# Fusing a distance-biased attention and an int4 map into one software-pipelined loop in written order

## The chip, the cores and the metric

The kernel runs on one core of a Trainium2 chip. A core has a tensor engine (PE, with its weight loads shown apart as PEld), a vector engine (DVE), a scalar engine (ACT), GpSimd (POOL) and a queue engine (SP) that issues most of the DMA transfers. The metric is device time in microseconds of a whole execution: median of three runs 1596.04 us, from 1595.28 to 1596.16.

## What is computed

The reference is a two-layer decoder with a layer norm after every residual, on 16 batches of 128 tokens of 256 numbers. Six parts follow each other, and the kernel has a stage for each:

```python
x = layernorm(x + moe(x))                    # stage 0: 8 experts, top 2, quantised weights
x = layernorm(x + attention(x, ctx, dist))   # stage 1: 16 heads of 16 numbers
x = layernorm(x + int4_map(x))               # stage 2
x = layernorm(x + state_space(x))            # stage 3
x = layernorm(x + attention(x, ctx, mask))   # stage 4
x = layernorm(x + expert_choice(x))          # stage 5
```

The parts that matter here, cut to their core:

```python
# stage 1
q = (query @ Wq.T + bq) * d ** -0.5;  k = ctx @ Wk.T + bk;  v = ctx @ Wv.T + bv
scores = einsum('bhqd,bhkd->bhqk', q, k) - log(distances + 1e-9) * abs(distance_scaling)
out = softmax(scores) @ v
return out @ Wo.T + bo
# stage 2
w = clip(round(kernel / scale), -8, 7) * scale       # scale = max(abs(kernel)) / 7
return x @ w + bias + (x @ a) @ b
```

## The kernel before

Everything is float32 in the stages concerned. A batch is one tile `x[b]` of 128 tokens (partitions) by 256. The instructions are traced in Python order, and a scheduler then chooses the order of each engine's instructions by its own costs and priorities, unless a block asks for the written order. An engine executes its list in order, each instruction waiting for the semaphores of what it needs.

**End of stage 0.** The experts' outputs are rows in a DRAM tensor `y_dram`. For each batch two indirect DMAs on POOL (L503) gather the two rows of every token into a tile of the tag `y`; DVE adds them with their weights (L507) and takes statistics (L508, L509); after four batches POOL computes the scales (L82, L83: power −0.5), and DVE normalises (L514). With `issue_after`, later gathers are held behind the scales of the group before.

**Stage 1** runs over 16 batches, in groups of four. `keys(g, c)` projects the context of four batches to keys; each key row is written twice (`mine`), once for the even and once for the odd head of a pair, the other head's rows zeroed, so that 32-row matmuls serve two heads (L623, L627). `values(b)` does the same for values (L634, L636), into one of three rotating tiles that hold zeros in the other head's columns. `turn(g)` transposes `x` (L101, L106), `queries(g)` projects it (L614, L615). `weights(b)` computes the scores (L649: four row groups of the array in turn), adds the bias `-log(dist)` (L655), takes the row maximum (L660) and exponentiates head by head (L662). `turn_weights(b)` transposes the 16 blocks of weights (L669) and copies them back in four pieces, two on DVE (L671) and two on ACT (L673). `attend1(b)` multiplies by the values (L680) and, with the constant matrix `sums`, adds up the weights (L688); DVE takes the reciprocal of 128x256 sums (L693) and multiplies (L695). `finish(b)` projects (L700), adds the residual (L702 on POOL, L703) and normalises (L88 to L93). The loop works on batch `b`, `b-1` and `b-2` in a turn, so three batches are in flight.

**Stage 2** comes after it: the int4 weights from the largest magnitude (L756 to L775), then for each batch a transposition, a product (L781), the residual (L783 on POOL, L784) and the normalisation.

[...]stage 1 has two tiles of two banks for the scores (`ps_s`), two banks `ps_m`, one `ps_t`, one `ps_o`. The weights of stages 3 and 4 (`load3`, `load4`) are loaded when the memory of stage 0 comes free; SP issues them from 271.28 us on.

Of the kernel before, what the change touches and what calls it, by code (L numbers as in the profile page):

```python
# [19 lines left out]
P = 128  # L20
# [98 lines left out]
def stage0(K, ahead):  # L119
# [3 lines left out]
    with ExitStack() as ctx:  # L123
# [152 lines left out]
        y_dram = K.new(dram, [NE * CAP, D], F32, "y_dram")  # L276
# [16 lines left out]
        for k in range(2):  # L293
# [4 lines left out]
            i = K.new(keep, [P, NB], U32, f"idx{k}")  # L298
# [3 lines left out]
            w = K.new(keep, [P, NB], F32, f"wt{k}")  # L302
# [189 lines left out]
        after = None  # L492
        for b0 in range(0, NB, 4):
            st = K.new(small, [P, 4, 6], F32, "ln_st4")
            mv = K.new(small, [P, 4, 2], F32, "ln_mv4")
            for i in range(4):
                b = b0 + i
                if i % 2 == 0:
                    g = K.new(work, [P, 5, D], F32, "y", bufs=2)
                for k in range(2):  # L500
                    gk = g[:, 2 * (i % 2) + k, :]
                    with tc.issue_after(after.ins) if after is not None and i >= 2 else ExitStack():
                        nc.gpsimd.indirect_dma_start(  # L503
                            out=gk, out_offset=None, in_=y_dram[:],
                            in_offset=bass.IndirectOffsetOnAxis(ap=idx[k][:, b:b + 1], axis=0),
                        )
                    nc.vector.scalar_tensor_tensor(x[b], gk, wt[k][:, b:b + 1], x[b], ALU.mult, ALU.add)  # L507
                nc.vector.bn_stats(st[:, i, :], x[b])  # L508
                nc.vector.bn_aggr(mv[:, i, :], st[:, i, :])  # L509
            rs = K.new(small, [P, 4], F32, "ln_rs4")  # L510
            after = K.rsqrt(small, rs, mv[:, :, 1:2].rearrange("p b c -> p (b c)"), 1.0, 1e-5, "ln_t4")
            for i in range(4):
                b = b0 + i
                nc.vector.tensor_scalar(x[b], x[b], mv[:, i, 0:1], rs[:, i:i + 1], ALU.subtract, ALU.mult)  # L514
# [36 lines left out]
def stage1(K, w, ctxT):  # L551
    tc, nc = K.tc, K.nc
    x = K.x
    with ExitStack() as ctx:
# [4 lines left out]
        ps = ctx.enter_context(tc.tile_pool(name="s1_ps", bufs=2, space=PSUM))  # L559
# [4 lines left out]
        nc.vector.memset(tiny, 1e-9)  # L564
        nds = K.new(keep, [P, 1], F32, "nds")
        nc.vector.tensor_scalar(nds, w.scale, -1.0, None, ALU.mult)
        nc.vector.tensor_tensor(nds, nds, w.scale, ALU.min)
        for g in range(4):
            bg = bias[:, 4 * g:4 * g + 4, :]
            nc.scalar.activation(bg, bg, AF.Ln, bias=tiny)  # L570
            nc.vector.tensor_scalar(bg, bg, nds, None, ALU.mult)


        pi = K.new(keep, [P, 1], I32, "pi")
        nc.gpsimd.iota(pi, pattern=[[0, 1]], base=0, channel_multiplier=1)
        nc.vector.tensor_scalar(pi, pi, 4, 1, ALU.logical_shift_right, ALU.bitwise_and)
        mine = K.new(keep, [P, 2], F32, "mine")
        nc.vector.tensor_copy(mine[:, 1:2], pi)
        nc.vector.tensor_scalar(mine[:, 0:1], mine[:, 1:2], -1.0, 1.0, ALU.mult, ALU.add)
        bq = K.new(keep, [P, KD], F32, "bq")  # L580
        nc.vector.tensor_scalar(bq, w.bq, HD ** -0.5, None, ALU.mult)
        bk = K.new(keep, [P, KD, 2], F32, "bk")
        for c in range(KD):
            nc.vector.tensor_scalar(bk[:, c, :], mine, w.bk[:, c:c + 1], None, ALU.mult)

        sums = K.new(keep, [P, 2, 2, HD], F32, "sums")
        nc.vector.memset(sums, 0.0)
        for j in range(2):
            nc.vector.memset(sums[:, j, j, :], 1.0)

        vals = [K.new(keep, [P, NH, 2, HD], F32, f"vals{i}") for i in range(3)]
        for t in vals:
            nc.vector.memset(t, 0.0)

        bo = K.new(keep, [P, D], F32, "bo_all")
        pb = K.new(ps, [P, D], F32, "ps_m")
        for k in range(KD):
            nc.tensor.matmul(
                pb, w.bv[:, k:k + 1].to_broadcast([P, P]), w.o[:, k, :], start=(k == 0), stop=(k == KD - 1),
            )  # L600
        nc.vector.tensor_tensor(bo, w.bo, pb, ALU.add)

        xT, qT, kT, s, oT = {}, {}, {}, {}, {}

        def turn(g):
            xT[g] = K.new(grp, [P, KD, 512], F32, "xT")
            K.transposed(ps, xT[g], x[4 * g:4 * g + 4], "ps_m")

        def queries(g):
            qT[g] = K.new(grp, [P, KD, 512], F32, "qT")  # L610
            for c in range(KD):
                pq = K.new(ps, [P, 512], F32, "ps_m")
                for k in range(KD):
                    nc.tensor.matmul(pq, w.q[:, k, c * P:(c + 1) * P], xT[g][:, k, :], start=(k == 0), stop=(k == 1))  # L614
                nc.scalar.activation(qT[g][:, c, :], pq, AF.Identity, scale=HD ** -0.5, bias=bq[:, c:c + 1])  # L615


        def keys(g, c):
            if c == 0:
                kT[g] = K.new(grp, [P, KD, 2, 512], F32, "kT")  # L620
# [90 lines left out]
        for b in range(NB + 2):  # L711
            g, i = divmod(b, 4)
            if b < NB:
                weights(b)
# [977 lines left out]
```

## Time and profile before

The profiled execution lasted 1598.8 us, at a mean granted PE clock of 0.922. The edges of the stages, from the timeline of the trace:

| stretch | us | PE busy | DVE busy | ACT busy | POOL busy |
|---|---|---|---|---|---|
| int4 map with the first squares of stage 3 | 480 to 521 | 27.84 | 21.02 | 13.06 | 23.87 |
| start of stage 3 | 521 to 560 | 24.35 | 29.96 | 12.11 | 5.27 |
| state space and memory | 560 to 780 | 203.71 | 148.39 | 88.75 | 99.38 |
| mostly attention with mask | 780 to 1179 | 375.80 | 193.05 | 186.01 | 95.78 |
| expert choice | 1179 to 1598 | 391.49 | 84.83 | 69.27 | 20.07 |

How to read the views that follow: the page gives, for 40 slices of some 40 us, the busy share of each engine in tenths, and the granted PE clock in tenths of full speed. An answer by stretches gives busy time and, in brackets, the number of instructions of each engine. A line of the timeline has start, duration, engine, source line, operation, output and inputs by the program's names, and in square brackets how long the engine was idle before and what released it. Matmuls are pipelined and their ends are modelled: a busy PE is not a PE at its peak. The start of one piece to the start of the next is the better measure, and the weight loads (PEld) show it.

### The profile page before, as it was taken

Reading aid. Unit: us, or ns where it says so; the run is one execution under the profiler, and the core shown is the slowest. Engines: PE = TensorE matmul, PEld = TensorE weight load, DVE = VectorE, ACT = ScalarE, POOL = GpSimd, SP = SyncE. Lnnn points to the kernel's source line nnn. Section 1 sums busy time; section 2 is a strip of 40 time slices with the busy share of each in tenths; the row PEclk is TensorE's granted clock in tenths of the full one; section 3 lists DMA queues with packets and bytes.
Section 4 is the critical chain, followed back from the end, with each engine's and each line's share of the span. In section 5 each row is a group of like instructions: output and inputs, shape, how many; then the busy total and the mean of one; then the engine's idle time right before and its main releaser. Section 6 shows DMA issues by size and latency. Waiting matters only on the chain. (4 is left out here: it accounts for less than half of the span.)

```text
span 1598.8 us, 18940 instructions
## 1 busy us (share of the span) xinstructions
PE 1355.1 (85%) x6925; PEld 887.7 (56%) x6925; DVE 823.8 (52%) x1692; ACT 630.3 (39%) x1642; POOL 349.7 (22%) x427
## 2 busy tenths in 40 slices
PE   3466645998987599989999999999887999999996
PEld 3243332555544266656655777777675555555554
DVE  4987756776875766774844444444713111131114
ACT  4577742565533344443222655545633111111110
POOL 2113145011115165533023221122311000000003
PEclk9778786999997799999899999999977999999998
DMA  7532125200000000000102100000000222222102
GB/s 240 170 127 96 42 79 97 85 1 1 2 1 1 0 1 1 0 1 1 53 0 107 52 1 1 1 1 1 1 1 0 69 86 92 91 72 79 66 14 66
DMA packets 49357, 71.99 MB, mean 45 GB/s; under 512 B 9552, under 2 KB 39216, under 8 KB 49008
## 3 DMA queue, kind: packets, MB, share of 16 engines
q1 hardware_dynamic: 47088, 65.24, 12.3%
q0 software_dynamic: 2176, 5.55, 1.7%
q8 instruction: 54, 0.88, 0.2%
q14 instruction: 39, 0.32, 0.1%
HBM read 60.77 MB, written 5.80 MB: 42 GB/s over the span
## 5 line engine op out<-in xcount | busy, mean ns | idle before, releaser
L1561 DVE TENSOR_TENSOR h<-h,ps_m 128x512 f32<-128x512 f32 x64 | 44.0, 687 | 254.2 <-PE ps_m L1558 254.2
L82 POOL TENSOR_SCALAR ln_t<-ln_mv 128x1 f32<-128x1 f32 (+1 forms) x84 | 16.3, 194 | 602.0 <-DVE ln_mv L90 592.5
L1558 PE MATMUL ps_m<-xin,l1f_upT 128*128 128x512 f32 x256 | 120.6, 592 | 0.0
L1555 PE MATMUL ps_g<-xin,l1f_gateT 128*128 128x512 f32 x256 | 120.6, 592 | 0.0
L1392 ACT ACTIVATE s<-s,m 128x128 f32<-128x128 f32 x256 | 99.0, 388 | 46.7 <-DVE m L1389 46.4
L1569 PE MATMUL ps_y<-l1f_downT,h 128*128 128x256 f32 x512 | 111.8, 379 | 0.0
L1560 ACT ACTIVATE h<-ps_g 128x512 f32<-128x512 f32 x64 | 38.2, 597 | 176.0 <-PE ps_g L1555 176.0
L1569 PEld LDWEIGHTS ps_y<-l1f_downT,h 128*128 128x128 f32 x512 | 97.3, 190 | 16.6 <-issue 3.8
L1396 POOL TENSOR_TENSOR s<-s,t 128x1024 f32<-128x1024 f32 x32 | 60.7, 1896 | 181.8 <-DVE t L1395 138.0
L662 ACT ACTIVATE s<-s,m 128x128 f32<-128x128 f32 x256 | 78.1, 389 | 40.6 <-DVE m L660 39.2
L1558 PEld LDWEIGHTS ps_m<-xin,l1f_upT 128*128 128x128 f32 x256 | 48.6, 190 | 59.5 <-issue 59.3
L1555 PEld LDWEIGHTS ps_g<-xin,l1f_gateT 128*128 128x128 f32 x256 | 48.6, 190 | 56.5 <-issue 56.0
L1298 PE MATMUL ps_m<-ctxT,l1x_W_k 128*128 128x256 f32 x256 | 61.1, 393 | 5.2 <-ACT ring L1301 4.7
L1423 PE MATMUL ps_m<-half,oT 128*128 128x256 f32 x256 | 61.0, 381 | 0.0
L1318 PE MATMUL ps_m<-l1x_W_v,ctxT 128*128 128x512 f32 x128 | 60.6, 618 | 0.0
L892 DVE SCALAR_TENSOR_TENSOR acc<-ps_m,l1a_conv_w,acc 128x508 f32<-128x508 f32 (+2 forms) x72 | 52.5, 734 | 11.0 <-ACT acc L888 10.9
L1298 PE MATMUL ps_m<-xT,half 128*128 128x256 f32 x256 | 57.5, 383 | 0.7 <-ACT xT L1364 0.7
L1298 PEld LDWEIGHTS ps_m<-ctxT,l1x_W_k 128*128 128x128 f32 x256 | 49.0, 196 | 13.8 <-ACT ring L1301 5.7
L649 PE MATMUL ps_s<-kT,qT 32*128 32x256 f32 x256 | 42.0, 463 | 16.6 <-DVE s L655 16.4
L93 DVE TENSOR_SCALAR x<-r,ln_mv,ln_rs 128x256 f32<-128x256 f32 x64 | 27.8, 435 | 54.6 <-POOL ln_rs L83 54.5
L1574 ACT COPY y<-ps_y 128x256 f32<-128x256 f32 x32 | 11.9, 372 | 110.8 <-PE ps_y L1569 63.1
L1298 PEld LDWEIGHTS ps_m<-xT,half 128*128 128x128 f32 x256 | 47.7, 190 | 8.5 <-ACT xT L1364 1.0
(426 smaller groups left out, 2982.3 us busy)
## 6 DMA issues: line engine op xcount, KB each, us to landing
w<-in_w_gate_dram SPq DMA_DIRECT2D x9, 1024.0 KB, 5.8
l1f_gateT<-in_l1f_gateT_dram SPq DMA_DIRECT2D x8, 1024.0 KB, 5.3
l1f_upT<-in_l1f_upT_dram SPq DMA_DIRECT2D x8, 1024.0 KB, 6.3
l1f_downT<-in_l1f_downT_dram SPq DMA_DIRECT2D x8, 1024.0 KB, 5.6
w<-in_w_down_dram SPq DMA_DIRECT2D x9, 512.0 KB, 6.6
ring<-y SPq DMA_DIRECT2D x128, 32.0 KB, 1.8
y_dram<-y SPq DMA_DIRECT2D x4, 640.0 KB, 3.3
x<-in_x_dram SPq DMA_DIRECT2D x16, 128.0 KB, 2.9
```

The costliest lines, as they stand in the source:

```text
L649: nc.tensor.matmul(pss[r // 2][:, r % 2, c, :, :], qT[g][rows, c, at], kT[g][rows, c, :, at], start=True, stop=True,)
L662: nc.scalar.activation(half[:, i, :], half[:, i, :], AF.Exp, bias=m[:, i:i + 1])
L892: nc.vector.scalar_tensor_tensor(accv[:, :, j:], pcv[:, :, :P - j], w.conv[:, c, TAPS - 1 - j:TAPS - j], accv[:, :, j:], ALU.mult, ALU.add,)
L1298: nc.tensor.matmul(pq[:, j, :], wt[k][:, at], src[:, k, :], start=(k == 0), stop=(k == KD - 1))
L1318: nc.tensor.matmul(pv, self.ctxT[:, k, b * P:(b + 1) * P], self.w.v[:, k, 512 * j:512 * j + 512], start=(k == 0), stop=(k == KD - 1),)
L1392: nc.scalar.activation(half[:, i, :], half[:, i, :], AF.Exp, bias=m[:, i:i + 1], accum_out=t[:, i:i + 1],)
L1396: nc.gpsimd.tensor_tensor(half, half, t.unsqueeze(2).to_broadcast([P, 8, P]), ALU.mult)
L1423: nc.tensor.matmul(py, oT[b][:, c, :], w.o[c // 4][:, c % 4, :], start=(c == 0), stop=(c == NC - 1))
L1555: nc.tensor.matmul(pg, w.gate[:, k, at], xin[:, k, e, :], start=(k == 0), stop=(k == KD - 1))
L1558: nc.tensor.matmul(pu, w.up[:, k, at], xin[:, k, e, :], start=(k == 0), stop=(k == KD - 1))
L1561: nc.vector.tensor_tensor(h, h, pu, ALU.mult)
L1569: nc.tensor.matmul(pd, hid[c][:, g * P:(g + 1) * P], w.down[:, c, :], start=(c == 0), stop=(c == FI // P - 1),)
```

## The change

The gathers' end of stage 0, stage 1 and stage 2 become one stage in which **all engines run in the written order** (`manual_schedule()` without a list of engines).

- `after_experts` returns four functions, `fetch`, `combine`, `scales` and `scaled`, that the new stage calls where it wants them. The tiles that live on (`idx`, `wt`, `y_dram`) move to pools that last longer. Gathers of six batches are issued first; those of batches 12 to 15 go into the first turns of the loop. The gathered rows have three buffers of their own (`got`).
- Keys of groups 0 to 2 and values 0 to 2 are projected ahead of the loop, the rest in turns 0 to 3. All 16 value tiles and all four key tiles are kept, so no buffer rotates. Their room is that of weights needed later: `load3` and `load4` are called after the stage, and each load waits until the last use of what stood there.
- The sums of the weights are no longer matmuls: POOL folds the 128 columns to 16 in three additions (`added`), DVE reduces the rest and takes the reciprocal of 128x16 numbers (`summed`), PE transposes those (`turn_sums`) and spreads them to 128x256 with a matrix of zeros and ones, `each` (`spread`). ACT copies the result to SBUF.
- Scores and bias are done by halves (`scores(b, h)`, `biased(b, h)`), on one score buffer; all four copies of transposed weights are on ACT, `ps_t` has two banks, `ps_m` four.
- Turn `n` of the loop works on five batches: scores and first exponentials of `n`, second exponentials of `n-1`, attention of `n-2`, residual and normalisation of `n-3`, int4 product of `n-4`. There are 20 turns.

It is meant to let the int4 map and the gathers run beside the attention, and to fix an order in which each engine has work of other batches while it waits.

```diff
-def stage0(K, ahead):
+def stage0(K, ahead, late, late_dram):
...
-                    with tc.issue_after(after.ins) if after is not None and i >= 2 else ExitStack():
-                        nc.gpsimd.indirect_dma_start(
...
+    def after_experts(work, small):
...
+        def fetch(b):
+            if b % 2 == 0:
+                got[b // 2] = K.new(work, [P, 4, D], F32, "got", bufs=3)
+            for k in range(2):
+                nc.gpsimd.indirect_dma_start(
...
-        ps = ctx.enter_context(tc.tile_pool(name="s1_ps", bufs=2, space=PSUM))
+        ps = ctx.enter_context(tc.tile_pool(name="s1_ps", bufs=4, space=PSUM))
+        ctx.enter_context(tc.manual_schedule())
+        fetch, combine, scales, scaled = after_experts(work, small)
...
+        parts = [t.rearrange("p a b -> p (a b)") for t in (room.inp, room.out, room.gate, own)]
+        vals = [t[:, 512 * i:512 * i + 512] for t, n in zip(parts, (5, 2, 2, 7)) for i in range(n)]
...
+        kT += [t.rearrange("p k (j n) -> p k j n", j=2) for t in (room.k, room.v)]
...
+        def scores(b, h):
...
+            pss[h] = K.new(ps, [P, 2, 2, 2, P], F32, "ps_s", bufs=1)
             for c in range(KD):
-                for r in range(4):
-                    rows = slice(32 * r, 32 * r + 32)
+                for i in range(2 * h, 2 * h + 2):
+                    rows = slice(32 * i, 32 * i + 32)
...
+        def added(b):
+            at, n = s[b].rearrange("p r c j k -> p (r c j) k"), P
+            while n > HD:
+                n //= 2
+                to = K.new(work, [P, NH, n], F32, f"sum{n}", bufs=1)
+                nc.gpsimd.tensor_tensor(to, at[:, :, :n], at[:, :, n:], ALU.add)
+                at = to
+                yield
+            ts[b] = at
...
-            pd = K.new(ps, [P, KD, P], F32, "ps_m")
-            for j in range(2):
-                for r in range(4):
-                    nc.tensor.matmul(
-                        pd[32 * r:32 * r + 32, :, :], sums[:, j, :, :].rearrange("p j d -> p (j d)"), s[b][:, r, :, j, :],
-                        start=(j == 0), stop=(j == 1),
-                    )
-            ri = K.new(work, [P, KD, P], F32, "ri")
-            nc.vector.reciprocal(ri, pd)
...
+        for b in range(6):
+            fetch(b)
...
+        for n in range(NB + 4):
...
+            if last:
+                residual("r", n - 3)
+                factor("r", n - 3)
+            if old:
+                summed(n - 2)
+                turn_weights(n - 2, 0)
+                turn_weights(n - 2, 1)
+                rest("r", n - 2, bo)
+            if new:
+                scores(n, 0)
+                biased(n, 0)
+            if prev:
+                exp(n - 1, 1, range(0, 2))
+            if old:
+                turned(n - 2, 0)
+                pn = turn_sums(n - 2)
+                turn_weights(n - 2, 2)
+            if prev:
+                exp(n - 1, 1, range(2, 4))
+            if old:
+                turned(n - 2, 1)
+            if last:
+                normed("r", n - 3)
+                rest("r2", n - 3, w2.bias)
+            if new:
+                largest(n, 0)
+            if end:
+                product("r2", n - 4, yT[n - 4], w2.kernel)
+            if prev:
+                exp(n - 1, 1, range(4, 6))
+            if old:
+                nc.scalar.copy(tT[n - 2], pn)
+                turned(n - 2, 2)
+                turn_weights(n - 2, 3)
+            if prev:
+                exp(n - 1, 1, range(6, 8))
+                sums = added(n - 1)
+                next(sums)
+            if old:
+                spread(n - 2)
+                turned(n - 2, 3)
+                nc.scalar.copy(ri[n - 2], pd[n - 2])
...
+            if n < 4:
+                combine(8 + 2 * n)
+            if new:
+                scores(n, 1)
+            if end:
+                residual("r2", n - 4)
+                factor("r2", n - 4)
+            if prev:
+                next(sums)
+                next(sums)
+                next(sums, None)
+            if last:
+                turn_again(n - 3)
+            if old:
+                attend1(n - 2)
+            if new:
+                biased(n, 1)
+                exp(n, 0, range(8))
+            if old:
+                nc.vector.tensor_tensor(oT[n - 2], po[n - 2], ri[n - 2], ALU.mult)
+            banks = []
+            if g < 3 and i == 1:
+                banks = list(turn(g + 1))
+            elif g < 3 and i > 1:
+                banks = list(queries(g + 1, i - 2))
...
+            if last:
+                nc.scalar.copy(yT[n - 3], pt[n - 3, "x"])
+            out_of(banks)
+            for b in ((3, 4, 5, 6), (7, 8, 9, 10), (11, 12, 13), (14, 15))[n] if n < 4 else ():
+                values(b)
+            if new:
+                largest(n, 1)
+            if old:
+                product("r", n - 2, oT[n - 2], w.o)
...
+            if end:
+                normed("r2", n - 4)
...
-def stage2(K, wts):
...
+                after_experts = stage0(K, ahead, late, late_dram)
...
+                stage1(K, w.one, w.two, w.ctxT, room, after_experts)
                 w.three, w.four = load3(K, p3), load4(K, p4)
-                stage1(K, w.one, w.ctxT)
-                stage2(K, w.two)
```

## The prediction

> **What bounds the kernel now.** I read the page's slices first, to see where the tensor engine is starved, then the busy time by stretches to put numbers on the stage that changes.
>
> ```profile
> PE   3466645998987599989999999999887999999996
> DVE  4987756776875766774844444444713111131114
> ACT  4577742565533344443222655545633111111110
> PEclk9778786999997799999899999999977999999998
> ```
> ```profile
> core 0: us, PE busy (x) PEld busy (x) DVE busy (x) ACT busy (x) POOL busy (x), PEclk, DMA share, GB/s
> 242.00:272.00 30.00, 12.55 (x42) 5.59 (x40) 15.81 (x46) 4.86 (x6) 18.83 (x21) 0.63 0.47 71
> 300.00:340.00 40.00, 39.82 (x279) 22.10 (x277) 27.86 (x43) 20.04 (x55) 5.35 (x11) 1.00 0.00 1
> 490.00:510.00 20.00, 13.43 (x45) 9.17 (x44) 9.66 (x31) 6.70 (x30) 14.66 (x29) 0.73 0.00 1
> ```
>
> A slice is 40 us. Stage 0 ends near 215, the int4 stage near 521. Between them lie three different regimes: the row gathers (215 to 272), in which no engine is full; the attention loop (272 to 473), in which PE is full and DVE, ACT and POOL are not; the int4 map (473 to 521), again with no engine full and the PE clock at 0.73. The timeline gives the edges and the cost of small pieces:
>
> ```profile
> 219.15 1.08 POOL L503 DMA_INDIRECT y<-y_dram,idx  x1 [4.62 <-DVE dist L571]
> 220.54 0.95 POOL L503 DMA_INDIRECT y<-y_dram,idx  x1 [0.30 <-issue]
> 258.18 1.19 DVE L655 TENSOR_TENSOR s<-ps_s,dist 128x1024 f32<-128x1024 f32 x1
> 271.70 1.18 DVE L660 TENSOR_REDUCE m<-s 128x8 f32<-128x1024 f32 x1
> 521.11 1.14 DVE L871 TENSOR_SCALAR xn<-x,rs 128x256 f32<-128x256 f32 x4
> ```
> ```profile
> 363.22 0.79 PEld L680 LDWEIGHTS ps_o<-s,vals 128*32 128x32 f32 x26 [0.33 <-DVE ln_st L88]
> 365.07 0.74 PEld L649 LDWEIGHTS ps_s<-kT,qT 32*128 32x128 f32 x14 [0.41 <-issue]
> 366.14 0.30 PEld L623 LDWEIGHTS ps_m<-ctxT,l0x_WkT 128*128 128x128 f32 x2 [0.33 <-issue]
> ```
> ```profile
> ACT s L662 <- DVE m L660: 32.9, 14, 5.4
> ACT s L673 <- PE ps_t L669: 24.2, 10, 5.7
> PEld ps_s L649 <- issue: 12.5, 39, 0.8
> PEld ps_o L680 <- issue: 9.4, 38, 0.8
> PEld ps_t L669 <- issue: 8.4, 27, 0.6
> ```
>
> Gathers are issued 1.25 us apart; the first row-maximum of attention (L660) waits until 271.70, because the combine steps of all gathers stand ahead of it on DVE. The reciprocals L693 run from 292.3 to 471.1 in 15 steps: **11.9 us a turn**. In the waits of 300 to 460, ACT waits for DVE and DVE and ACT wait for PE, while PE's own losses are "issue": 0.33 to 0.41 us each time the shape of the array tile changes (128*128, 128*32, 32*128), some 124 times in 13.4 turns, 3.3 us a turn. First work of the next stage is xn at 521.11.
>
> **What the Trainium skill says.** "TensorEngine Tiling (Array Packing)", Key Properties: changing the tiling mode drains the engine. The trace agrees (those 0.33 to 0.41 us). "TensorE: Matmul & The Clock Gate", What's actually happening: PE runs at half clock after an idle window and returns to full after some 3.4 us of work. The trace agrees: granted 0.50 in 270 to 280, 1.00 from 290 on. "GPSIMD Engine Reference", Elementwise: two-input operations on GpSimd are held by one read port. Here a 128x1024 product takes 1.90 us (L1396) or 2.36 (L966); I use the first and keep the second for the range.
>
> **The change, part by part.** One turn of the loop is costed per engine, from rows of before.
>
> PE, pieces: a transpose of 128 columns 0.107 us (four L669 in 0.42); a 256-column record 0.218 (L1569: 111.8/512), two records a matmul; 32-wide attend records 0.026 (26 in 0.68); scores 0.053 (14 in 0.74, four row groups at once). Before, a turn: transposes 1.7, scores 0.85, attend 0.85, sums 0.85, values 0.85, keys 0.85, queries 0.85, output 0.85, turn 0.2: 7.9, plus 3.3 drains, plus small waits: 11.9, which checks the method. After: the sums' matmuls go (−0.85), keys and values leave the loop (−1.7), the int4 product and its turn come in (+1.05), a transpose of the sums and their spreading come in (+0.55). The scores are issued by halves, with two row groups in flight instead of four: 8 records at 0.107, twice: 1.7 instead of 0.85. Sum 6.7. Written order leaves seven mode changes a turn (into scores, to the sums, back, into spread, out of scores, into attend, out): 7 × 0.36 = 2.5. So 9.2; with turn (0.86 in one turn of four) and queries (1.7 in two of four) 10.3. Without them the output product waits for oT: 0.2 + 0.4 + 0.2, so 10.0.
>
> ACT: 16 exponentials 4.8 (L662 x16 in 4.78), four copies of 128x512 2.3, tT 0.2, ri and yT 0.37 each, banks 0.65 on average: 8.7. DVE: adds and maxima 4 × 1.17 = 4.7, sums' reduce and reciprocal 0.5, oT 0.35, two residuals with statistics 1.85, two normalisations 0.75: 8.1. The 1.76 us reciprocal (L693), the two ps_t copies and the value copies are gone. POOL: three folds 1.9 + 1.1 + 0.73 (the line through 256: 0.73 and 1024: 1.90), two rests 1.46, two factors of 0.85: 6.9; with 2.36 for the widest fold 7.5. PE is the longest, **10.3 us a turn**.
>
> Can waits in written order push a turn beyond that? The exponentials of half 1 stand first on ACT in the next turn, behind the maximum, behind oT, behind attend, behind the last ps_t copy. From that copy: attend 1.3, semaphores 0.3, oT 0.4, maximum 1.2: 3.2 us. In the same time ACT does ri, eight exponentials and yT: 3.2. It closes without a gap. summed stands ahead of the next bias add on DVE and needs POOL's third fold: it ends some 0.4 us before. That is the thinnest place. ps_m has four banks; each of the six or seven tiles of a turn finds the fourth before it already read. The int4 weights' preparation (5.6 us in the trace from 472.8 to 480.8) goes among the gathers, where DVE idles; I cost it, the memsets and the keys at nothing there.
>
> Prologue: 12 gathers from 219 to 234; combine(3) ends 232, its scales wait for POOL, 235.5, scaled(0) 237; turn and first queries with the cold clock 7 us; scores 245, first bias add **246** (combine(7) ends 244.6 on DVE). Turns 0 to 3 carry keys(3), 13 values (0.9 us of PE, 0.5 of ACT each) and eight combines: 10, 9, 12, 12, so turn 4 starts at 289. Turns 4 to 15: 8 × 10.4 + 4 × 10.0 = 123: 412. Four draining turns 7 + 6 + 5 + 3 = 21: 433. The next stage had its squares (L866, 0.61 each) done beside the int4 map; now four of them and a 1.2 us scale may stand after it: +3. So 436 instead of 521: **−85 us**. The weights of the following stages land later, as their room holds keys and values until turns 6 to 15, but all well ahead of their use: nothing. Stages 3 to 5 only shift. 1596 − 85 = **1511**.
>
> **The rivals.** (A) As above, PE sets 10 to 10.5 us. (B) Written order saves nothing in a turn: drains or the POOL fold leave 11.9, and the gain is only the int4 stage and the earlier start: 289 + 12 × 11.9 + 21 + 3 = 456: 1531. For it speaks that the best case needs two chains to close within 0.4 us, and 7.9 us of PE work took 11.9 before. (C) Drains overlap with loads and ACT is the bound, 8.7: 286 + 104 + 18 = 408: 1483. Against it: every mode change in the trace showed its gap. (D) **Slower**: the engines wait for each other in turn, DVE and ACT alternate, 8.1 + 8.7 = 17 us a turn: 246 + 48 + 204 + 30 + 4 = 532: 1607. For it: strict order has no work to fill a late maximum, ps_s has a single buffer, and an unfilled PE falls to the half clock. Against it: each engine has work of four other batches in every turn.
>
> **How the numbers follow.** A 0.60, B 0.20, C 0.12, D 0.08. The time is A's. The range takes A and B, the dearer fold and half of C: 1483 to 1550. D is 0.06 slower, 0.01 about equal and 0.01 still faster. So faster 0.93, same 0.01, slower 0.06.
>
> **What would show it.** Right: first L655-like add near 246; its starts 10 to 10.5 us apart in turns 4 to 15; PE clock 1.0 in them; no stretch like 490 to 510 with clock 0.73 longer than 20 us; xn near 436. Wrong: long waits of ACT for the half-1 maximum, of DVE for the folds of POOL, or a PE clock below 0.8 inside the loop; or a late load of in_proj before the next stage.

## The result: 1517.5 us, and the profile after

| | us, median | lowest to highest | ratio to before (95% interval) |
|---|---|---|---|
| before | 1596.10 (4 runs) | 1595.28 to 1599.65 | |
| after | 1517.51 (4 runs) | 1511.58 to 1518.24 | 0.9495 [0.9467, 0.9523] |

The change takes 78.6 us off. The forecast was 1511, its range 1483 to 1550. The profiled executions last 1598.8 us before and 1516.3 us after, and nearly all of the difference lies ahead of stage 3: its first normalised rows (`xn`) stand at 521.11 before and at 436.79 after, 84.3 us earlier. What follows takes 1077.7 us before (1598.8 − 521.1) and 1079.5 us after (1516.3 − 436.8). So only the new stage is to be explained.

The page's slices, some 38 us each now, on the same four rows as before:

```profile
PE   3456578899857999889999999999779999999995
DVE  5987768989866677667435443455422111211114
ACT  4576875778834444332226545545423111111110
PEclk9877698989988999999899999999959999999998
```

Slices 8 to 11, counted from 1, lie wholly in the loop. DVE stands at 8 and 9 there and ACT at 7 and 8; in the loop before (slices 8 to 12) they stood at 6 to 8 and at 3 to 6. The weak stretch that was the int4 map is gone. The stage by stretches; the columns are busy time with the number of instructions in brackets, and the granted PE clock:

```profile
core 0: us, PE busy (x) PEld busy (x) DVE busy (x) ACT busy (x) POOL busy (x), PEclk, DMA share, GB/s
242.00:272.00 30.00, 25.09 (x123) 15.63 (x123) 25.98 (x44) 19.55 (x61) 19.89 (x21) 0.94 0.36 60
283.00:296.30 13.30, 13.11 (x89) 9.40 (x90) 11.70 (x21) 8.50 (x26) 8.16 (x10) 0.75 0.01 1
296.30:310.40 14.10, 10.16 (x80) 7.42 (x79) 11.38 (x19) 8.40 (x26) 7.98 (x11) 0.75 0.00 1
300.00:340.00 40.00, 34.84 (x297) 25.00 (x289) 34.60 (x61) 28.99 (x86) 25.43 (x33) 0.87 0.10 34
340.00:400.00 60.00, 54.93 (x552) 40.45 (x551) 57.22 (x105) 54.25 (x160) 48.66 (x62) 1.00 0.12 37
```

From 242 to 272 PE was busy for 12.55 us and is now busy for 25.09: the keys, values and first turns run while rows are still gathered. From 340 to 400 PE, DVE and ACT are each busy for over nine tenths of the time, and the clock is full. From 300 to 340 the clock is 0.87, and in the two turns from 283.0 to 310.4 it is 0.75: the early turns have gaps, of which more below. The edges, from the timeline (start, duration, engine, line, operation):

```profile
246.85 1.23 DVE L688 TENSOR_TENSOR s<-ps_s,dist 128x1024 f32<-128x1024 f32 x1
436.79 1.15 DVE L1042 TENSOR_SCALAR xn<-x,rs 128x256 f32<-128x256 f32 x4 [2.70 <-POOL rs L83]
```

L688 is the bias add that opens a turn (L655 before). The starts of the first half's add, one a turn, measure the loop. After turn 0 at 246.85 the gaps are 12.3, 11.0, 12.9, 13.3, 14.1, 10.4, 9.1, 10.4, 9.9, 8.6, 9.3, 9.1, 8.5, 8.4 and 8.7 us. Late turns take 9.1 us where they carry queries and **8.5 where they don't**; the last five average 8.81.

One late turn on PE, from its weight loads. The brackets give PE's idle time before a piece and what ended it:

```profile
382.42 0.73 PEld L758 LDWEIGHTS ps_m<-l0x_WoT,oT 128*128 128x128 f32 x4 [1.08 <-DVE oT L919]
...
384.35 0.73 PEld L681 LDWEIGHTS ps_s<-l1x_W_v,qT 32*128 32x128 f32 x8 [0.17 <-issue]
385.87 0.09 PEld L730 LDWEIGHTS ps_m<-ident,t 128*16 128x16 f32 x1 [0.79 <-DVE t L717]
...
388.89 0.20 PEld L781 LDWEIGHTS ps_m<-ident,x 128*128 128x128 f32 x2 [0.33 <-DVE r L765]
...
390.96 0.30 PEld L758 LDWEIGHTS ps_m<-l0x_WoT,oT 128*128 128x128 f32 x2 [0.89 <-DVE oT L919]
```

`l1x_W_v` names the memory of a later weight, in which keys are kept here. From 382.42 to 390.96 is one turn of 8.54 us: about 6.0 us of loads, 0.84 us of gaps that go with a change of the array's shape (0.17 into the scores, into the spreading and into attend, 0.33 ahead of the turn of `x`), and two waits for DVE, 0.79 for the reciprocal of the sums (L717) and 0.89 for `oT` (L919).

The waits of the late loop (310 to 403), in us in total, times, longest:

```profile
PEld ps_m L758 <- DVE oT L919: 5.9, 5, 1.8
ACT s L700 <- DVE m L695: 5.1, 6, 1.4
...
PEld ps_m L747 <- issue: 1.7, 10, 0.2
```

Of the 32.9 us for which ACT waited for row maxima before (in a longer stretch of 160 us), 5.1 are left in 93 us, and the gap into attend (L747) is 0.17 (1.7 us in 10), where it was 0.33 in the line of before (L680).

### The profile page after: what moved, and what is told of

It reads as the page before. It is cut to its first block, busy times and chain, and to the rows that moved or that the text cites. A ratio compares the mean times of both kernels' runs of the same rounds, so it can differ in the third digit from the quotient of the medians.

```text
span 1516.3 us, 18650 instructions
## 1 busy us (share of the span) xinstructions
PE 1298.2 (86%) x6742; PEld 874.4 (58%) x6749; DVE 802.6 (53%) x1648; ACT 658.3 (43%) x1722; POOL 422.3 (28%) x477
## 5 line engine op out<-in xcount | busy, mean ns | idle before, releaser
L1563 ACT ACTIVATE s<-s,m 128x128 f32<-128x128 f32 x256 | 99.0, 388 | 46.4 <-DVE m L1560 46.2
L1567 POOL TENSOR_TENSOR s<-s,t 128x1024 f32<-128x1024 f32 x32 | 60.7, 1896 | 183.5 <-DVE t L1566 158.7
L700 ACT ACTIVATE s<-s,m 128x128 f32<-128x128 f32 x256 | 83.3, 394 | 14.7 <-DVE m L695 14.7
L1745 ACT COPY y<-ps_y 128x256 f32<-128x256 f32 x32 | 11.9, 372 | 110.8 <-PE ps_y L1740 73.9
L1469 PEld LDWEIGHTS ps_m<-ctxT,l1x_W_k 128*128 128x128 f32 x256 | 49.9, 200 | 14.1 <-ACT ring L1472 5.7
L1556 DVE TENSOR_TENSOR s<-ps_s,hide 128x1024 f32<-128x1024 f32 x32 | 39.0, 1221 | 23.3 <-PE ps_s L1552 21.5
L83 POOL TENSOR_TENSOR ln_rs<-ln_t,mhalf 128x1 f32<-128x1 f32 (+1 forms) x84 | 48.7, 580 | 7.0
```

Of the source, the lines that this page charges most:

```text
L83: return self.nc.gpsimd.tensor_tensor(out, t, self.mhalf[: out.shape[0], :n], ALU.pow)
L700: nc.scalar.activation(at, at, AF.Exp, bias=m[h][:, i:i + 1])
L1469: nc.tensor.matmul(pq[:, j, :], wt[k][:, at], src[:, k, :], start=(k == 0), stop=(k == KD - 1))
L1563: nc.scalar.activation(half[:, i, :], half[:, i, :], AF.Exp, bias=m[:, i:i + 1], accum_out=t[:, i:i + 1],)
L1567: nc.gpsimd.tensor_tensor(half, half, t.unsqueeze(2).to_broadcast([P, 8, P]), ALU.mult)
```

## Experiments

All are made from the kernel after, one edit each. Theory A is that PE's queue sets a late turn, C that ACT does. The expectations call A "T", the tensor engine, and their "D" is that DVE sets the turn (in the last of them, that the planner moves DVE or ACT work ahead of what PE waits for); that is not the prediction's rival D. P ("port"), formed on the profile after, is that DVE operations which use only SBUF are held up while POOL adds up the weights, and that this is what makes the early turns long. Which of them are held up is seen below. The first time is the start of the first bias add; "six turns" is from it to the seventh turn; "late turn" is the mean of the last five gaps. The kernels in the written order, but for e6_gathers_first, have nearly the same work ahead of the first add, and it starts between 244.9 and 250.9: a difference of a few us there says little.

| kernel | median us | ratio to before (95%) | first add | six turns | late turn | xn at |
|---|---|---|---|---|---|---|
| after | 1517.51 | 0.9495 [0.9467, 0.9523] | 246.9 | 73.9 | 8.81 | 436.8 |
| e1_short_fold | 1500.07 | 0.9396 [0.9369, 0.9423] | 244.9 | 65.2 | 8.66 | 421.9 |
| e2_pe_more | 1524.01 | 0.9535 [0.9517, 0.9552] | 248.7 | 75.5 | 9.67 | 448.3 |
| e3_act_more | 1515.99 | 0.9493 [0.9477, 0.9509] | 246.1 | 72.0 | 8.86 | 434.5 |
| e4_dve_more | 1525.66 | 0.9543 [0.9525, 0.9560] | 245.6 | 73.1 | 9.13 | 444.7 |
| e6_gathers_first | 1531.62 | 0.9590 [0.9569, 0.9611] | 273.7 | 62.6 | 8.81 | 451.8 |
| e7_int4_after | 1540.47 | 0.9635 [0.9617, 0.9652] | 247.1 | 74.1 | 7.91 | 461.8 |
| e8_sums_matmul | 1546.03 | 0.9673 [0.9656, 0.9691] | 246.3 | 76.0 | 12.24 | 468.1 |
| i1_spread | 1522.48 | 0.9528 [0.9509, 0.9546] | 247.6 | 70.8 | 8.83 | 442.3 |
| i2_before_fold | 1530.98 | 0.9586 [0.9573, 0.9599] | 249.2 | 87.5 | 8.76 | 452.0 |
| i3_norm_later | 1530.54 | 0.9584 [0.9571, 0.9597] | 250.9 | 83.9 | 8.84 | 451.3 |
| e5_free_order | 1587.34 | 0.9947 [0.9928, 0.9966] | 262.6 | 83.8 | 13.61 | 505.7 |
| e9_pe_order | 1605.69 | 1.0064 [1.0048, 1.0080] | 262.9 | 94.3 | 14.96 | 526.6 |

### What sets a late turn: a little more work on one engine

**PE.** The int4 product is done twice.

```diff
+            if name == "r2":
+                for k in range(KD):
+                    nc.tensor.matmul(py[name, b], lhs[:, k, :], rhs[:, k, :], start=(k == 0), stop=(k == 1))
```

> The changed kernel with the int4 product of each batch issued twice into the same bank: four more 256-column records, 0.87 us of PE a turn, 16 times. Theory T (PE sets the turn): 0.87 x 16 = 14 us slower than the changed kernel, 1531. Theory D (DVE sets the turn, with PE waiting 0.6 to 1.0 us a turn for oT where there are no queries): only the turns with queries or a turn of x pay, some 0.3 to 0.5 us each: 3 to 6 us, 1521 to 1524.

The late turn goes from 8.81 to 9.67 us, +0.86: all of it is paid. The first six turns, two of which hold the product, take 1.6 more; two of the turns between pay nothing (10.39 and 8.63 us, against 10.41 and 8.63). The time rises by 6.5 us, `xn` of the profiled execution is 11.5 later. That lies between the forecasts of T (14) and D (3 to 6): it is the last five turns that speak, not the time.

**ACT.** Two of its copies are done twice.

```diff
                 nc.scalar.copy(ri[n - 2], pd[n - 2])
+                nc.scalar.copy(ri[n - 2], pd[n - 2])
...
                 nc.scalar.copy(yT[n - 3], pt[n - 3, "x"])
+                nc.scalar.copy(yT[n - 3], pt[n - 3, "x"])
```

> The changed kernel with the copies of ri and of yT each done twice: 0.37 + 0.35 = 0.72 us of ACT more in a turn, 16 times. If ACT sets the turn: 11.5 us slower than the changed kernel, 1529. Theory D (DVE): ACT waits 0.5 to 1.0 us a turn for the half-1 maximum in turns without banks and not at all in the others; about a third is paid, 3 to 5 us, 1521. Theory T: about the same as D, since the last ps_t copy, and with it attend, comes at most 0.4 us later: 3 to 6 us.

Nothing: a late turn of 8.86, and the time within the interval of the kernel after, where every theory had forecast 3 us or more. ACT is busy for 80.51 of 92.47 us in the late loop and still has room for 0.72 us a turn.

**DVE.** The statistics are taken twice.

```diff
             nc.vector.bn_stats(st, r[name, b])
+            nc.vector.bn_stats(st, r[name, b])
```

> The changed kernel with the statistics of each of the two residuals taken twice: 2 x 0.43 = 0.86 us of DVE more in a turn, 16 times. Theory D (DVE sets the turn: busy 8.3 of 8.5 us in turns 12 to 15): 0.8 x 16 = 13 us slower than the changed kernel, 1530. Theory T (PE): DVE has slack only in the turns with queries; in the others oT comes later and PE waits longer: 4 to 7 us, 1522 to 1525.

Of 0.86 us more a turn, 0.32 are seen in a late turn; the time rises by 8.1 us, where T had 4 to 7 and D 13. PE's two waits for DVE, 0.79 and 0.89, are part of its turn: DVE can delay PE through them, though it doesn't set the turn alone. Together the three runs speak for A: **PE's queue sets the late turn**, with its waits for DVE in it.

### What each part of the change is worth: one undone

**The gathers.** All combine steps and scalings stand ahead of the loop.

```diff
+        scaled(1)
+        combine(8)
+        combine(9)
+        fetch(12)
...
-            if n < 4:
-                combine(8 + 2 * n)
```

> The changed kernel with all gathers, combines and normalisations of stage 0 ahead of the loop, as it was before the change; keys, values and the rest stay. It prices the spreading of the gathers over the first turns. 32 gathers at 1.25 us from 219.8 on end near 263, the last combine and scaling near 269, so the first bias add comes at about 270 instead of 246.8 (+23). Theory P (port): without combines beside the folds, turns 0 to 5 take about 9.5 each instead of 12.3, 11.0, 12.9, 13.3, 14.1, 10.4 (-17): in all +4 to +10, 1521 to 1527. Theory without P (combines cost only their own 1.35 us in a turn): -8 in the turns, in all +15, 1532.

The first bias add is 26.8 us later, and the first six turns, relieved of that work, are 11.3 shorter; `xn` is 15.0 later. Running the last gathers beside the loop hides 15 us of 27; the rest is paid in longer early turns. P had forecast 17 us off the turns and 1521 to 1527, the theory without P 8 off and 1532: by its time this run is against P, by its turns between the two.

**The int4 map.** It runs after the loop, in a written order of its own.

```diff
-        for n in range(NB + 4):
+        for n in range(NB + 3):
...
+        for n in range(NB + 2):
+            if 0 <= n - 2:
+                normed("r2", n - 2)
+            if n < NB:
+                rest("r2", n, w2.bias)
+                turn_again(n)
...
```

> The changed kernel with the int4 map taken out of the loop and run as a pass of its own over the 16 batches behind it, in written order, three batches in flight. It prices the fusion. The loop's late turns lose 1.1 us of PE (product and transposition): 8.5 to about 7.6 if PE sets them; the pass costs about 2 us a batch with the PE at half clock, 32 to 36 us, less the 3 us of the last draining turn. Sum -15 + 35 - 3 = +17: 1534 (1526 to 1542). If DVE set the turn, the loop would fall by 1.4 us a turn: +9, 1526.

A late turn is 0.9 us shorter, about what PE's product and turn of `x` cost (0.73 and 0.20 of loads in the kernel after), and nothing of what leaves the other engines shows: once more PE. `xn` is 25.0 later. The first six turns are no shorter (74.1 against 73.9); from the first bias add to the last turn's the loop is 6.6 us shorter, and the drain by about as much: attention's last normalisation stands at 419.80, the map's last at 433.10 in the kernel after and at 458.06 here. So the map costs some 13 us in the loop and saves a pass of some 38.

**The sums.** They are matmuls with a matrix of ones again, and DVE takes the reciprocal of 128x256; POOL adds nothing.

```diff
-                summed(n - 2)
...
+                nc.vector.reciprocal(ri[n - 2], pd[n - 2])
                 nc.vector.tensor_tensor(oT[n - 2], po[n - 2], ri[n - 2], ALU.mult)
```

> The changed kernel with the sums of the weights as matmuls with the constant matrix again, and the reciprocal of 128x256 numbers on DVE (1.76 us), as before the change; folds, turn_sums, spread and the ri copy go. PE: +0.85 and a drain, less 0.75: about +0.4 a turn; DVE +1.1; and the reciprocal stands between attend and oT, for which PE waits. Theory T (the chain of PE and oT sets the turn): late turns 8.5 to about 10.2; Theory P: early turns lose the stretched operations, some 12 us in all. Sum +24 - 12 = +12: 1529 (1520 to 1538). If the folds cost nothing: 1540.

The late turns are not alike here, and 12.24 us is the mean of 10.66, 10.67, 11.95, 13.95 and 13.96: from 332 to 386 the granted clock is 1.00, from 398 to 426 it is 0.74. Timeline of DVE in one of the longest:

```profile
405.14 1.76 DVE L921 RECIPROCAL ri<-ps_m 128x256 f32<-128x256 f32 x1 [1.04 <-PE ps_m L750]
```

The reciprocal waits 1.04 us for the sums and takes 1.76, and only behind it come `oT` and the next row maximum; ACT waits 17.8 us for maxima in 350 to 426. The way by sums of 128x16 on POOL and DVE is worth 28 us (1546.0 − 1517.5), where 12 were forecast. Nor are the early turns shorter (76.0), though POOL adds nothing here and the scalings take 444 ns in the mean: whether the reciprocal took back what P had promised, the run can't tell.

**The written order.** First the planner orders every engine.

```diff
-        ctx.enter_context(tc.manual_schedule())
```

> The same loop without the written order: the planner that ordered the rest of the kernel orders this stage on all engines. If the written order is what makes the five-turn batches cheap, the drains of PE between tiling modes come back to 0.36 us each, the turn goes from 8.7 to 10 us and more, and the kernel takes 1540 us or more. If the saving comes from one loop alone (no second pass over the block, no own stage for the int4 map), the time stays within 1505 to 1530.

Then it orders all but PE.

```diff
-        ctx.enter_context(tc.manual_schedule())
+        ctx.enter_context(tc.manual_schedule(engines={mybir.EngineType.PE}))
```

> The written order is kept on PE alone; the planner orders the other engines. If PE's order is all that counts (theory A: PE sets the turn), 1505 to 1525, with late turns of 8.5 to 9.1 us. If the planner moves DVE or ACT work of another turn ahead of what PE waits for (theory D), the turns grow to 10 us and more, and the kernel takes 1535 us or more.

The same loop with the planner's order is 70 us slower and only 0.53% better than before. With PE's instructions in the order of the kernel after, it is 88 us slower and 0.64% **worse than before**. Both are within 1% of before. So PE's order alone doesn't make the loop pay; the order of the engines that feed it does. Whether it would without PE's isn't tested. Nor are the changes of the array's shape the reason, which the first expectation had at 0.36 us again: under the planner the gap into attend is 0.17 us as well (1.7 us in 10) and that into the scores 0.30 (2.7 in 9) against 0.17, tenths of a us in turns that are 4.8 us longer. The late loop by stretches, ten turns of each kernel, after first and then with PE's order alone:

```profile
310.40:402.87 92.47, 86.18 (x823) 63.00 (x823) 86.78 (x156) 80.51 (x236) 71.25 (x89) 0.98 0.12 39
```
```profile
340.70:486.50 145.80, 108.92 (x823) 78.25 (x823) 87.06 (x156) 81.80 (x236) 73.18 (x91) 0.81 0.07 24
```

The same 823 PE, 156 DVE and 236 ACT instructions; DVE's busy time differs by 0.28 us, ACT's by 1.3. All that is added is waiting, and then PE pays a second time: with its clock at 0.81 the same matmuls take 108.92 us in place of 86.18. Where the waiting comes from is seen in one turn of the kernel with PE's order alone, DVE first:

```profile
446.44 0.42 DVE L715 TENSOR_REDUCE tot<-sum 128x16 f32<-128x256 f32 x1 [3.12 <-POOL sum L708]
...
449.81 0.41 DVE L919 TENSOR_TENSOR oT<-ps_m,ri 128x256 f32<-128x256 f32 x1
450.14 1.21 DVE L695 TENSOR_REDUCE m<-s 128x8 f32<-128x1024 f32 x1
```

and in the same turn ACT and PE:

```profile
451.39 0.69 ACT L700 ACTIVATE s<-s,m 128x128 f32<-128x128 f32 x2 [5.33 <-DVE m L695]
```
```profile
450.28 2.07 PE L758 MATMUL ps_m<-l0x_WoT,oT 128*128 128x256 f32 x4 [5.42 <-DVE oT L919]
452.15 1.91 PE L723 MATMUL ps_t<-ident,s 128*128 128x128 f32 x8
```

DVE's row sum L715 was put ahead of the statistics, and stands still for 3.12 us until POOL's third addition is done. Behind it wait the statistics, the normalisation, the second bias add, `oT` and the row maximum. PE stands for 5.42 us for `oT`, ACT for 5.33 for the maximum, and then eight transpositions take 1.91 us, at a granted clock of 0.50 from 450 to 455, where they take 1.04 in the kernel after (383.38). From 357 to 486, DVE's waits for POOL in this kernel (in all, times, longest):

```profile
DVE tot L715 <- POOL sum L708: 21.0, 8, 3.3
DVE x L776 <- POOL ln_rs L83: 15.5, 17, 0.9
```

That is 36.5 us, and in the late loop of the kernel after DVE's waits for POOL are too short to be listed. By the rates of the two stretches above, this one is longer by an estimated 47 us (129 − 129 × 92.47 / 145.80). In the kernel after, the row sum stands behind the statistics and directly ahead of the next turn's bias add, where POOL is already done:

```profile
385.14 0.39 DVE L715 TENSOR_REDUCE tot<-sum 128x16 f32<-128x256 f32 x1
...
385.73 1.16 DVE L688 TENSOR_TENSOR s<-ps_s,dist 128x1024 f32<-128x1024 f32 x1
```

No bracket: no wait. That the place of this one row sum explains all 70 to 88 us isn't shown: no run moved it alone, the planner also moved scales and gathers on POOL and the preparation on DVE, and the first bias add comes 16 us later in both kernels.

### Why the early turns are long

The lines that gave theory P, from the timeline of the kernel after:

```profile
298.58 2.36 POOL L708 TENSOR_TENSOR sum<-s 128x1024 f32<-128x1024 f32 x1
298.86 3.20 DVE L524 TENSOR_SCALAR x<-x,ln_mv,ln_rs 128x256 f32<-128x256 f32 x4
304.56 1.65 PE L758 MATMUL ps_m<-l0x_WoT,oT 128*128 128x256 f32 x3 [3.94 <-DVE oT L919]
```

Four normalisations, 1.45 us elsewhere (249.24), take 3.20 beside POOL's widest addition, and PE, for which `oT` comes late behind them, idles for 3.94. This turn is the one of 14.1 us. PE's granted clock is at 0.50 from 303.5 to 313.5, and was from 283.0 to 289.7, behind a gap of 2.39 us in its loads: over the first six turns it is 0.86. So the early turns pay for waits and for the clock.

**Hardly any fold.** POOL adds two blocks of 16 columns once, in place of three additions over 128.

```diff
-            while n > HD:
-                n //= 2
-                to = K.new(work, [P, NH, n], F32, f"sum{n}", bufs=1)
-                nc.gpsimd.tensor_tensor(to, at[:, :, :n], at[:, :, n:], ALU.add)
...
+            nc.gpsimd.tensor_tensor(to, at[:, :, :HD], at[:, :, HD:2 * HD], ALU.add)
```

> The changed kernel, but POOL folds only columns 0 to 15 with 16 to 31 (one addition of 128x256, 0.74 us) instead of all 128 columns in three additions (2.37 + 1.28 + 0.74 us), so the sums leave out 96 of 128 keys. Nothing else changes. Theory P (port): DVE operations with two SBUF inputs or on SBUF alone are stretched while POOL folds; they then fall back: the normalisation L776 from 0.57 us mean to about 0.42, the combine L510 from 0.66 to about 0.5; turns 2 to 5, which take 12.9 + 13.3 + 14.1 + 10.4 = 51 us now, fall to about 44, late turns from 8.6 to about 8.2; in all 8 to 14 us faster than the changed kernel (1503 to 1510). Theory T (tensor engine sets the turn, as predicted): the folds are hidden, at most 3 us faster (1514 or more).

17 us faster than the kernel after, more than P had forecast. `xn` is 14.9 earlier: 2.0 at the first add, which may be chance, 8.7 in the first six turns, the rest in later turns and the drain; the late turn changes by 0.15 only. PE's clock over the first six turns is 0.92. The DVE operations are quick again, the scalings and the combines from 246 to 434, in the kernel after first, then in this one (total, mean ns of one):

```profile
L524 DVE TENSOR_SCALAR x<-x,ln_mv,ln_rs 128x256 f32<-128x256 f32 x12 | 6.1, 570 | 0.0
L510 DVE SCALAR_TENSOR_TENSOR x<-got,wt,x 128x256 f32<-128x256 f32 x16 | 13.9, 867 | 0.3
```
```profile
L524 DVE TENSOR_SCALAR x<-x,ln_mv,ln_rs 128x256 f32<-128x256 f32 x12 | 4.5, 435 | 0.0
L510 DVE SCALAR_TENSOR_TENSOR x<-got,wt,x 128x256 f32<-128x256 f32 x16 | 7.9, 495 | 0.3
```

The other normalisations go from 567 ns to 430 (groups of L776, here L775). So POOL's additions do slow DVE, but not all of it, and P as it stands is too wide. Row maxima (L695) and statistics (L767) use only SBUF too, and are as long beside an addition as without one: 1.21 and 1.22 us, 0.43 and 0.43, for 26 and 20 of the 32 of each. In the kernel after:

```profile
382.28 1.21 DVE L695 TENSOR_REDUCE m<-s 128x8 f32<-128x1024 f32 x1
382.80 2.08 POOL L708 TENSOR_TENSOR sum<-sum 128x512 f32<-128x512 f32 x2
```

Held up are the scalings, the other normalisations and the combines. Whether moving DVE's work away from POOL's additions recovers the time is another question, and three versions asked it. "GPSIMD Engine Reference", Specifications, says that GpSimd shares its SBUF interfaces with DVE and contends with DVE instructions in a two-port mode or with two SBUF inputs; the trace agrees for the combines, which have two SBUF inputs, and adds the size; which mode the scalings ran in it doesn't show.

**One combine a turn**, scalings in pairs.

```diff
-            if n < 4:
-                combine(9 + 2 * n)
+            if n < 8:
+                combine(8 + n)
...
+            if n in (4, 5):
+                scaled(2, range(2 * (n - 4), 2 * (n - 4) + 2))
```

> The changed kernel with the combines of batches 8 to 15 one a turn over turns 0 to 7 instead of two a turn over 0 to 3, and the normalisations of groups 2 and 3 two batches a turn (turns 4, 5, 8, 9) instead of four at once (2, 4). Same work. Theory P: the four scalings at once (3.20 us beside a fold) kept PE idle for 3.9 us and threw its clock to half; without such a heap turn 4 falls from 14.1 to about 11, turns 1 to 3 from 37.2 to about 32, turns 5 to 8 rise by about 1 each: -5 to -9 in all, 1509 to 1513. If the load of DVE alone counts: no difference within 3 us.

The expectation missed: 5 us slower. The first six turns are 3.1 shorter, the following four 7.3 longer (45.4 against 38.1). In this kernel:

```profile
296.23 2.56 DVE L524 TENSOR_SCALAR x<-x,ln_mv,ln_rs 128x256 f32<-128x256 f32 x2
```

Two scalings lose as much as four did: 2.56 against 0.72 is 1.8 more, 3.20 against 1.45 is 1.75 more. POOL's widest addition runs from 295.94 to 298.31, and DVE stands until it ends. In these two cases the loss is one for each meeting, not one for each operation, and spreading makes more meetings: the scalings were held once in the kernel after, and four times here, 1.8 us each. The time held in the four later turns is some 3.7 us longer; the rest of their 7.3 isn't explained.

**All of it behind the first bias add**, ahead of the row maximum.

```diff
                 biased(n, 0)
+            if n in (0, 2, 4):
+                scaled(1 + n // 2)
+            if n < 4:
+                combine(8 + 2 * n)
+                combine(9 + 2 * n)
```

> Both combines and the scalings of turns 0 to 4 stand on DVE right behind the bias add of the first half, where GpSimd has no fold to do; their number and kind are unchanged. If theory P is right (DVE operations on buffers alone stand still while GpSimd folds), the scalings cost 4 x 0.42 us again instead of 3.2, the turns 0 to 4 lose 6 to 10 us in sum, and the kernel takes 1508 to 1512 us. If it is rather the DVE work itself that the early turns pay (it is only moved here, ahead of the maxima of the half), the time stays at 1517, or rises to about 1525, because the maxima and with them the exponentials come later.

Missed again, 13 us slower, nearly all of it in the first turns (87.5 against 73.9 us). The DVE of turn 1:

```profile
266.63 3.72 DVE L510 SCALAR_TENSOR_TENSOR x<-got,wt,x 128x256 f32<-128x256 f32 x2
...
272.51 1.19 DVE L695 TENSOR_REDUCE m<-s 128x8 f32<-128x1024 f32 x1
```

The fold had moved too: it waits for the exponentials, which had become later, and met the combine all the same (266.32 to 268.66). And the maximum now comes 7 us after the bias add at 265.49, where in the kernel after it follows at once (259.11, 260.37). In 246 to 310 ACT waits 18.4 us for maxima here, in the kernel after 8.9, and PE's clock over the first six turns is 0.80.

**The same, and the int4 map's normalisation away from the fold.**

```diff
+            if 0 <= n - 5:
+                normed("r2", n - 5)
             if last:
                 normed("r", n - 3)
...
-            if end:
-                normed("r2", n - 4)
```

> As i2_before_fold, and the normalisation of the int4 map (128x256, buffers alone) stands one turn later, ahead of the other normalisation, instead of at the turn's end beside the 512-wide fold. Theory P: it takes 0.42 instead of 0.66 to 0.82 us; in the late turns PE sets the pace, so no gain there beyond 0.1 us a turn: 1506 to 1512, at most 4 below i2_before_fold. If DVE does set late turns, 16 x 0.3 = 5 us below i2_before_fold; one normalisation more stands in the drain (+0.5).

The forecast missed here too. The hold is gone from the normalisations and the scalings, but not from the combines. The groups of 246 to 434:

```profile
L776 DVE TENSOR_SCALAR x<-r,ln_mv,ln_rs 128x256 f32<-128x256 f32 x26 | 9.8, 413 | 0.1
L524 DVE TENSOR_SCALAR x<-x,ln_mv,ln_rs 128x256 f32<-128x256 f32 x12 | 4.1, 406 | 0.0
L510 DVE SCALAR_TENSOR_TENSOR x<-got,wt,x 128x256 f32<-128x256 f32 x16 | 12.9, 807 | 0.3
```

413 and 406 ns, and yet 1530.5 us, no better than i2_before_fold, with a late turn of 8.84. That settles one thing: in late turns the held normalisation costs nothing, as it would if PE sets the pace. For the early turns it shows that **getting away from the fold isn't enough**: what was put between a bias add and its maximum cost more than the hold that went. It doesn't show what the early turns would take without the hold, because the combines, 807 ns in the mean against 867, are held almost as before. The fold costs the early turns about 9 us in all (e1_short_fold); how much of it is the hold and how much is that the sums, and what waits for them, come later isn't told apart. None of the three versions beats the kernel after.

## Why the prediction was right, and where its terms were off

- **The mechanism held.** One loop, PE as the engine that sets a late turn (A, at 0.60), the int4 map and the gathers largely hidden in it, stages 3 to 5 only shifted. The first add came at 246.85 where 246 was forecast, `xn` at 436.79 where 436 was.
- **Two signs did not come.** Turns 4 to 15 were to start 10 to 10.5 us apart: of the eleven gaps from 296.27 on two do (10.4 each), one is 14.1 and the others are 8.4 to 9.9. The clock was to be 1.0 in them, and below 0.8 inside the loop was named as a sign of being wrong: it is 0.75 in turns 3 and 4, and 1.00 only from 314 on.
- **Two errors cancelled inside, and that the time came within 7 us is in part luck.** Turns 0 to 3: forecast 10 + 9 + 12 + 12 = 43, measured 49.4 (246.85 to 296.27), +6.4. Turns 4 to 15: forecast 123, measured some 115 (296.27 to 402.87 is eleven turns, 106.6, and one more of 8.7), −8. Drain: forecast 21, measured 21.5 (to the last normalised `x`, which starts at 433.10).
- **The term that was too large: seven changes of shape at 0.36.** In the late turn shown PE loses 0.17 three times and 0.33 once, 0.84 instead of 2.5; of the other changes two fall into the waits for DVE, and one, back from the transposed sums (385.87 to 385.88), shows no gap. The price was too high for the kernel before as well: PE's waits named "issue" from 300 to 460 sum to 39.2 us in 131, which is 0.30 apiece and 2.9 a turn, not 3.3. Why a change costs less in the new loop is open; for attend it isn't PE's written order, since the gap is 0.17 under the planner too. "TensorEngine Tiling (Array Packing)", Key Properties, says that a change drains the engine; the trace shows gaps at most of the changes, and none at one. Against this, PE waits 1.68 for DVE, where 0.8 was counted. The scores by halves were priced at 1.7 a turn: the loads of the first half take 0.73, and those of the second share 0.74 with the spreading.
- **The term that was too small: DVE in the early turns.** Combines and scalings were counted at their own durations, with no price for standing beside POOL or in front of `oT`. With them ahead of the loop (e6_gathers_first) the turns of 12.9 to 14.1 take 11.3, 10.3 and 8.5. That PE's clock would fall in them was given no price either.
- **POOL's folds** measured 2.37 + 1.28 + 0.75 = 4.4 us, where 1.9 + 1.1 + 0.73 was taken. The dearer 2.36, kept for the range, was the right row for the widest. POOL doesn't set a turn, but the "thinnest place", the row sum that waits for the third fold, is where the planner's order breaks.
- **Rival B** (11.9 a turn, 1531) fell: 8.81. **Rival C** (8.7 a turn, 1483) met the length of a late turn with the wrong reason: changes of shape are cheaper than A took them, as C said, but ACT takes 0.72 us more a turn without a trace. The time was not C's, since early turns average over 12 us.
- **Rival D** (engines wait for each other in turn, 1607, slower) was given 0.08. Its time, though not its reason, the written order, is that of the same loop when DVE, ACT and POOL are left to the planner: 14.96 us a turn and 1605.69 us. The argument against it, that each engine has work of four other batches in every turn, was true in that run too and didn't help when the instruction in front had to wait.
- **The rest** is confirmed in sum only: keys, memsets and the int4 weights' preparation among the gathers in a first add that is 0.85 late; the later loads and the shift of stages 3 to 5 in 1079.5 against 1077.7; the squares, set at +3, in the 3.7 from the last normalised `x` to `xn` (one takes 0.42 us in the trace before, L866, where 0.61 was taken). Of what is quoted on the clock, the trace before shows the two levels, not the 3.4 us: from 270 to 280 PE was busy for 5.95 of 10 us and still at 0.50.

## What to carry to other kernels

In a software-pipelined loop price not only each engine's work but what stands at the head of its queue: a short instruction that waits 3 us holds everything behind it, and the engines fed by it lose more, PE twice, by idling and by its clock. Ordering the engine that is the bound was not enough here; order those that feed it too, and try putting an instruction that waits for a slow neighbour behind all that others wait for. Before moving work away from a slow meeting, look at what it is moved in front of.

## What the runs showed of the hardware

- Scalings and combines on DVE stood until a POOL addition beside them ended: 128x256 scalings, 0.36 us apiece, took 2.56 for two and 3.20 for four beside an addition of 2.37 us, and two combines 3.72 beside additions in a row, where two take 0.97 without one (i2_before_fold, 266.63 and 270.94). Bias adds, which read PSUM, went on undisturbed (1.19 to 1.23 us for 13 beside an addition, 1.16 to 1.23 for 19 without), and so did row maxima, which don't (1.21 us for 26).
- POOL's addition of two 128x1024 operands takes 2.37 us (mean of 16), where the product with one number for each row of 128, L1567 on the page, takes 1.90. It isn't repeated numbers as such: the product L966 of before, whose second operand is one 128x128 block used eight times, takes 2.36.
- PE's matmuls are dearer in a loop with gaps than in one without: ten late turns' matmuls took 108.92 us at a granted clock of 0.81 and 86.18 at 0.98. The clock was at 0.50 with and after waits of 3.94 us (303.5 to 313.5) and 5.42 us (450 to 455 in e9_pe_order), and stayed at 1.00 through waits of up to 1.8 us in the late loop.
